# Depthwise products on 8 channels at four shifts, side by side on TensorE; natural channel order of x; the fractional part's transfers by halves

## The chip, the core and the metric

The kernel runs on one core of a Trainium2 chip. A core has five engines that run side by side and meet at semaphores: TensorE (matrix products; PE in the profile, its weight loads PEld), VectorE (DVE), ScalarE (ACT), GpSimd (POOL) and SyncE (SP), which here issues the transfers. Sixteen DMA engines move the data. SBUF is the working memory of 128 partitions; TensorE writes its results to PSUM, eight banks on the same 128 partitions. The metric is the device time of one execution in microseconds (us).

## The reference

The input `x` is 32 x 96 x 56 x 56 (images, channels, rows, columns), and two layers follow each other. Each layer works on its input normalised over groups of three channels (`_gn`) and is added to that input:

```
def _gn(v, G=32, eps=1e-5):
    g = v.reshape(B_, G, C_ // G, H_, W_)
    m = jnp.mean(g, axis=(2, 3, 4), keepdims=True)
    s = jnp.var(g, axis=(2, 3, 4), keepdims=True)
    return ((g - m) / jnp.sqrt(s + eps)).reshape(v.shape)
...
x = x + _L0_conv_ref(_gn(x), ...)
x = x + _L1_conv_ref(_gn(x), ...)
return x
```

The first layer is a quantised inverted bottleneck: a 1x1 convolution expands 96 channels to 576; batch normalisation and a 4-bit activation follow; then a depthwise 3x3 convolution (each of the 576 channels on its own, padding 1), the same two after it, and a 1x1 convolution back to 96 with batch normalisation. All three weights are quantised to 4 bits.

The second layer splits the channels into three parts of 32. The first part goes through a 3x3 convolution with gated weights, the second through a fractional Fourier transform over rows and columns, a gated 1x1 mix of real and imaginary parts, the inverse and the absolute value, the third through an ordinary Fourier transform with a gated mix and back. The parts are joined and go through a dense 3x3 convolution, 96 to 96.

## The kernel before

All images go through one program for the whole run; nothing is looped on the chip. For each image the code makes a list of steps in three streams: `head` (load, statistics, normalised input `hi`/`lo`), `body` (first layer) and `rest` (second layer). `arrange` interleaves the streams of neighbouring images, so that the second layer of image i stands beside the first layer of image i+1. `Order` then takes the recorded instructions, their true dependences, and a model of each instruction's duration (`Order.model`), and lays down a fixed order for each engine by list scheduling. The order on the chip is the result of that planner; DMAs are all issued by SP in such a fixed order too.

**First layer.** Pixels are held by parity: a channel's 56 x 56 plane is four planes of 28 x 28 (u = 0 to 3 for row and column parity), each with a border, 872 bytes (`QS`) in fp8. The 576 hidden channels come in five blocks (b) of 128, the last of 64.
- `expand(b, u)`, L684: four f32r products per parity into a PSUM pair of banks; `quant_act` (L633) has ScalarE apply scale, offset and relu to 8-bit codes, and VectorE shift and mask them in `q1s` (partition = channel).
- `leave(b, u)`, L702, writes `q1s` to DRAM (`sd`); `enter(b, h)`, L710, reads it back so that a partition is one of 32 channels x 4 parities: tile `d`, 128 partitions, two groups of 32 channels to a tile, three buffers.
- `depthwise(b, g)`, L718: for a group of 32 channels the 3x3 convolution on parity planes is a product with a 128 x 128 weight matrix (input parity and channel by output parity and channel) at four shifts of the plane: (0,0), (0,1), (1,0), (1,1). Four products of 392 columns accumulate in one bank; there are two halves. So 18 groups x 8 = 144 products per image, 4608 in all. ScalarE and VectorE quantise the pair of banks to `q2s`.
- `leave2` and `enter2` (L734, L741) take the result through DRAM (`gd`) to `q2`, channels on partitions, and `project(u)` (L744) makes the output and adds it to `x`.
The pool of PSUM pairs has two buffers, which expand, depthwise and project share.

**Second layer.** `norm` (L821) normalises the middle channels into a part of `F` and waits for the last product of the image before. `leave_x`/`enter_x` (L828, L832) turn that part through DRAM from channels on partitions to rows on partitions (`xh`). `forward_h`, `forward_w`, `inverse_w` and `inverse_h` are the transform; `leave_pq`/`enter_pq` (L984, L988) turn its result back into `F`, in one piece. `mix_f` (L1003) multiplies `F` by the gated weights: its products have 32 columns of weights, and for j = 0 to 3 write to PSUM partitions 32j to 32j + 31 of one bank. `mix_t` (L1065) does likewise. `spatial` (L1084) is the gated 3x3 convolution. The three parts meet in `cat`; `winograd` (L1106) and `final` (L1140, products on L1145) make the dense convolution and add it to `x`, and `store` (L1192) writes it out.

The channels of `x` lie on the partitions in the order 64 to 95, 32 to 63, 0 to 31 (`groups`, L441), so that `load` and `store` need three DMAs of 32 partitions for each quarter of a plane.

The products that the change is about:

```
for half in range(2):
    for t in range(4):
        nc.tensor.matmul(
            ps[:, half, :HN],
            dw[n][:, t, :],
            view(s["d"][b, g], PQ * (14 * half + t // 2) + t % 2, [[PQ, 14], [1, HH]]),
            start=(t == 0),
            stop=(t == 3),
        )
```

Of the kernel before, what the change touches and what calls it, by code (L numbers as in the profile page):

```python
# [63 lines left out]
NB = 5  # L65
# [74 lines left out]
class Order:  # L140
# [16 lines left out]
    def needs(self, tiles):  # L157
# [3 lines left out]
        for k, access in enumerate(self.access):  # L161
            for a, w in access:
# [10 lines left out]
                if m not in past:  # L173
                    past[m], free[m] = [], set()
                    if m in tiles:
                        pool, tag, bufs = tiles[m]
                        row = tags.setdefault((pool, tag), [])
                        if len(row) >= bufs:
                            free[m] |= users[row[-bufs]]
                        elif pool in ("p1", "p3"):  # L180
                            free[m] |= early
                        if row:
                            free[m].add(first[row[-1]])
                        first[m] = k
                        row.append(m)
# [19 lines left out]
    def model(self):  # L205
# [3 lines left out]
        for i, e, access in zip(self.ins, self.eng, self.access):  # L209
# [6 lines left out]
            if i.opcode == "DMACopy":  # L216
                took = 0.55 if e == "SP" else 0.4
                size = _bytes(outs[0].dtype)
                for _, c in outs[0].ap:
                    size *= c  # L220
                move = size / 200e3
                for a in (outs[0], ins[0]):
                    run = _bytes(a.dtype)
                    for step, c in reversed(a.ap):
                        if step * _bytes(a.dtype) == run or c == 1:
# [3 lines left out]
                    if run < 512:  # L229
                        move *= 1.4  # L230
                        break
                lag = 1.0 + move
            elif e == "PE":
# [7 lines left out]
                else:  # L241
                    took = max(cols / 2350.0, 0.05)
            elif e == "Activation":
# [177 lines left out]
def block_kernel(ctx: ExitStack, tc: tile.TileContext, out: bass.AP, a: dict):  # L421
# [19 lines left out]
    groups = ((0, 2 * G), (G, G), (2 * G, 0))  # L441
    xts = {}

    def load(i):
        xt = xp.tile([C, HW], F32, tag="x", name=f"x{i}")
        for at in range(0, HW, 2 * HN):
            for p, c in groups:
                src = x_in[i, c : c + G].rearrange("c h w -> c (h w)")
                nc.sync.dma_start(out=xt[p : p + G, at : at + 2 * HN], in_=src[:, at : at + 2 * HN])
# [12 lines left out]
    with tc.tile_pool(name="prep", bufs=1) as pp:  # L462
# [35 lines left out]
        eye = load_tmp("eye32")  # L498
        dw = []
        for g in range(NQ):  # L500
            d = cp.tile([128, 4, 128], FP8, tag=f"dw{g}", name=f"dw{g}")
            nc.vector.tensor_tensor(
                view(d.rearrange("p s m -> p (s m)"), 0, [[128, 4], [4, 32], [1, 4]]),
                view(w2, 16 * g, [[4, 4], [0, 32], [1, 4]]),
                view(eye, 0, [[0, 4], [1, 32], [0, 4]]),
# [59 lines left out]
    p1 = Pool(ctx.enter_context(tc.tile_pool(name="p1", bufs=1)), "p1", 1, tiles)  # L565
    p3 = Pool(ctx.enter_context(tc.tile_pool(name="p3", bufs=3)), "p3", 3, tiles)
# [78 lines left out]
    def layer0(i):  # L645
# [56 lines left out]
        def leave(b, u):  # L702

            n = blk(b) // 32
            if u == 0:
                s["sd", b] = dp.tile([n, 32, 4, QS], FP8, tag=f"sd{n}", name=f"sd{i}_{b}")
            q = q1s[(NB * i + b) % 2]
            nc.sync.dma_start(out=s["sd", b][:, :, u, :].rearrange("g c n -> c g n"), in_=q[: blk(b), u, :])

        def enter(b, h):  # L710

            d = p3.tile([128, 2, QS], FP8, tag="d", name=f"d{i}_{b}_{h}")
            src = s["sd", b][2 * h : 2 * h + 2].rearrange("g c u n -> (c u) g n")
            nc.sync.dma_start(out=d, in_=src)
            for g in range(2):
                s["d"][b, 2 * h + g] = d[:, g, :]

        def depthwise(b, g):  # L718
            n = 4 * b + g
            ps = pair(f"pd{i}_{n}")  # L720
            for half in range(2):
                for t in range(4):
                    nc.tensor.matmul(  # L723
                        ps[:, half, :HN],
                        dw[n][:, t, :],
                        view(s["d"][b, g], PQ * (14 * half + t // 2) + t % 2, [[PQ, 14], [1, HH]]),
                        start=(t == 0),
                        stop=(t == 3),
# [5 lines left out]
        def leave2(b, g):  # L734

            n = blk(b) // 32
            if g == 0:
                s["gd", b] = dp.tile([32, n, 4, 2 * HN], FP8, tag=f"gd{n}", name=f"gd{i}_{b}")
            nc.sync.dma_start(out=s["gd", b][:, g], in_=s["q", b, g])

        def enter2(b):  # L741
            nc.sync.dma_start(out=q2[b][: blk(b)], in_=s["gd", b].rearrange("c g u n -> (c g) u n"))
# [73 lines left out]
    def layer1(i):  # L816
# [11 lines left out]
        def leave_x():  # L828
            s["xd"] = dp.tile([G, HW], F32, tag="xd", name=f"xd{i}")
            nc.sync.dma_start(out=s["xd"], in_=s["F"][2 * G : 3 * G])  # L830

        def enter_x():  # L832

            s["xh"] = p1.tile([2 * H, G // 2, W], F32, tag="h", name=f"xh{i}")
            for q in range(2):
                src = s["xd"][G // 2 * q : G // 2 * (q + 1)].rearrange("c (h w) -> h c w", w=W)
                nc.sync.dma_start(out=s["xh"][H * q : H * (q + 1)], in_=src)

        def norm1():
# [3 lines left out]
            nc.vector.tensor_scalar(s["T"][:G], xts[i][:G], mean[:G], rstd[:G], ALU.subtract, ALU.mult)  # L843

        def norm0(u):
# [3 lines left out]
                view(xts[i][2 * G : C], W * (u // 2) + u % 2, [[2 * W, HH], [2, HH]]),  # L849
                mean[2 * G : C],  # L850
                rstd[2 * G : C],
# [116 lines left out]
        def inverse_h(g):  # L968
# [8 lines left out]
            if g < 4:  # L977
                dst = view(pq, 4 * W * g, [[2 * W, 2], [G // 2 * W, 2], [1, 2 * W]])
# [5 lines left out]
        def leave_pq():  # L984
            s["pd"] = dp.tile([2 * H, G + 1, W], F32, tag="pd", name=f"pd{i}")
            nc.sync.dma_start(out=s["pd"], in_=s["pq"])

        def enter_pq():  # L988
            for q in range(2):
                src = s["pd"][H * q : H * (q + 1)]  # L990
                nc.sync.dma_start(
                    out=s["F"][G * q : G * (q + 1)].rearrange("c (h w) -> c h w", w=W),
                    in_=src[:, :G, :].rearrange("h c w -> c h w"),
                )
                nc.sync.dma_start(
# [494 lines left out]
```

## Time and profile before

| | |
|---|---|
| median of 3 runs | 3622.18 us (3622.07 to 3627.27) |
| the profiled execution | 3621.32 us, its span 3619.5 us |
| VectorE, its two largest groups | L638: 232.5 us (640, mean 371 ns) and 150.3 us (576, mean 273 ns) |
| ScalarE, its two largest groups | L636: 628.9 us (640, mean 1003 ns) and 578.3 us (576, mean 1004 ns) |
| DMA | 406.08 MB in 491611 packets, mean 112 GB/s |
| granted TensorE clock | 0.947 of full speed, mean |

How to read the profile's lines: a group names its line in the code, the engine, the operation, output tiles <- input tiles, shapes, and the count; then its busy time (overlaps within the group counted once), the mean duration of one in ns, and the idle time of the engine just before them with what ended it. A TensorE record lasts until its result is written, so records of products that follow each other overlap; how long one holds the array is the distance to the next one's start. An f32 product stands in the records twice. In the timeline a row is a run of equal instructions: start, length from the first start to the last end, engine, line, operation, tiles, shapes, count.

### The profile page before, as it was taken

What the parts mean: (1) busy time and instruction counts of PE and PEld (TensorE: products, weight loads), DVE (VectorE), ACT (ScalarE), POOL (GpSimd) and SP (SyncE); (2) the same over time, 40 slices, a digit from 0 to 9 for tenths busy, and PEclk for the clock granted to TensorE, in tenths of its full rate; (3) what the DMA queues carried; (4) which work ended last, traced back from release to release, by engine and by line L of the source; (5) the groups of instructions that cost most, each with busy time, mean ns of one, the idle gap of its engine ahead of it and who ended that gap; (6) DMA issues with size and microseconds to landing.
All of it is one profiled execution on the core that took longest, in us unless ns stands there. A gap on an engine that the chain in (4) does not pass through costs nothing. (4 is left out here: it accounts for less than half of the span.)

```text
span 3619.5 us, 50492 instructions
## 1 busy us (share of the span) xinstructions
PE 3326.5 (92%) x17024; PEld 2059.6 (57%) x17024; DVE 2458.2 (68%) x5553; ACT 2109.3 (58%) x2792; POOL 584.3 (16%) x657
## 2 busy tenths in 40 slices
PE   3799999999999999999999999999999999999987
PEld 2555565556565555565555565555655555655554
DVE  6457676667667667667676766676676676766765
ACT  3566555566556566555566656566555665555542
POOL 3111110111101111101111101111101111101100
PEclk9899999999999999999999999999999999999997
DMA  4344444444454444444444444444444444444332
GB/s 109 103 120 120 113 121 112 108 123 113 116 123 112 106 124 112 115 123 103 108 124 114 118 122 103 114 123 113 117 123 102 118 119 110 124 112 107 101 91 48
DMA packets 491611, 406.08 MB, mean 112 GB/s; under 512 B 221094, under 2 KB 443288, under 8 KB 490328
## 3 DMA queue, kind: packets, MB, share of 16 engines
q1 hardware_dynamic: 487168, 400.10, 44.1%
q10 hardware_dynamic: 4184, 2.75, 0.3%
q8 instruction: 135, 2.21, 0.3%
q14 instruction: 124, 1.02, 0.1%
HBM read 202.71 MB, written 199.97 MB: 111 GB/s over the span
## 5 line engine op out<-in xcount | busy, mean ns | idle before, releaser
L723 PE MATMUL pd<-d,dw 128*128 128x392 fp8e4 x4608 | 1026.7, 358 | 62.8 <-DMA d<-sd 60.3
L636 ACT ACTIVATE q2s<-pd,o,s 128x784 uint8<-128x784 f32 x576 | 578.3, 1004 | 628.8 <-PE pd L723 620.2
L1145 PE MATMUL pc<-V,wcw 96*96 96x392 f32 x2304 | 887.3, 495 | 9.3 <-DVE V L1122 9.3
L636 ACT ACTIVATE q1s<-pe,o,s 128x784 uint8<-128x784 f32 (+1 forms) x640 | 628.9, 1003 | 285.1 <-PE pe L689 283.0
L723 PEld LDWEIGHTS <-dw 128*128 128x128 fp8e4 x4608 | 468.2, 104 | 551.5 <-issue 276.8
L689 PE MATMUL pe<-hi,w1r 96*128 96x392 f32 x1280 | 526.2, 415 | 97.8 <-ACT q1s L636 70.8
L1145 PEld LDWEIGHTS pc<-V,wcw 96*96 96x96 f32 x2304 | 374.7, 164 | 213.6 <-issue 173.2
L689 PE MATMUL pe<-lo,w1r 96*128 96x392 f32 x1280 | 471.1, 368 | 3.3 <-POOL lo L680 2.9
L638 DVE TENSOR_SCALAR q1s<-q1s 128x218 uint32<-128x218 uint32 (+1 forms) x640 | 232.5, 371 | 257.5 <-ACT q1s L636 252.1
L689 PEld LDWEIGHTS pe<-hi,w1r 96*128 96x128 f32 x1280 | 243.0, 192 | 237.9 <-ACT q1s L636 141.0
L638 DVE TENSOR_SCALAR q2s<-q2s 128x196 uint32<-128x196 uint32 x576 | 150.3, 273 | 238.0 <-ACT q2s L636 227.4
L680 POOL TENSOR_TENSOR lo<-v,hi 96x784 fp32r<-96x784 f32 x128 | 238.2, 1861 | 258.0 <-ACT hi L679 241.2
L689 PEld LDWEIGHTS pe<-lo,w1r 96*128 96x128 f32 x1280 | 246.7, 193 | 52.0 <-issue 16.8
L748 PE MATMUL pp<-q,w3q 128*96 128x392 fp8e4 x1280 | 244.0, 333 | 18.9 <-DMA q<-gd 8.3
L628 POOL TENSOR_TENSOR stb<-veb,mhalf 96x1 f32<-96x1 f32 x32 | 23.2, 726 | 1324.2 <-DVE veb L627 1324.2
L748 PEld LDWEIGHTS <-w3q 128*96 128x96 fp8e4 x1280 | 151.1, 124 | 107.5 <-issue 41.5
L679 ACT CAST hi<-v 96x784 fp32r<-96x784 f32 x128 | 107.7, 841 | 174.0 <-DVE v L676 173.3
L758 DVE SCALAR_TENSOR_TENSOR x<-pp,s,x 96x392 f32<-96x392 f32 x256 | 145.4, 617 | 72.9 <-PE pp L748 70.8
L1022 POOL COPY cat<-sq 32x392 f32<-32x392 f32 x256 | 144.9, 566 | 287.2 <-ACT sq L1018 278.7
L1088 PE MATMUL ps<-s,g 128*128 128x392 f32 x512 | 187.7, 502 | 0.0
L1102 ACT ACTIVATE cat<-ps,b 32x392 f32<-32x392 f32 x256 | 162.5, 636 | 16.3 <-PE ps L1088 12.1
L676 DVE TENSOR_SCALAR v<-x,sta 96x784 f32<-96x784 f32 x128 | 89.6, 700 | 101.3 <-POOL lo L680 79.9
(158 smaller groups left out, 4393.5 us busy)
## 6 DMA issues: line engine op xcount, KB each, us to landing
d<-sd SPq DMA_DIRECT2D x288, 218.0 KB
gd<-q2s SPq DMA_DIRECT2D x576, 98.0 KB
sd<-q1s SPq DMA_DIRECT2D x512, 109.0 KB
q<-gd SPq DMA_DIRECT2D x128, 392.0 KB
x<-in_x_dram SPq DMA_DIRECT2D x384, 98.0 KB
out_dram<-x SPq DMA_DIRECT2D x384, 98.0 KB
pd<-pq SPq DMA_DIRECT2D x32, 808.5 KB
F<-pd SPq DMA_DIRECT2D x64, 392.0 KB
```

Of the source, the lines that this page charges most:

```text
L636: nc.scalar.activation(dst, ps, AF.Relu, bias=offset, scale=scale)
L638: nc.vector.tensor_scalar(w, w, 4, 0x0F0F0F0F, ALU.logical_shift_right, ALU.bitwise_and)
L679: nc.scalar.copy(s["hi"][:, u, :], v)
L680: nc.gpsimd.tensor_tensor(s["lo"][:, u, :], v, s["hi"][:, u, :].bitcast(F32), ALU.subtract)
L689: nc.tensor.matmul(ps[:, half, :HN], w1[:, 128 * b : 128 * (b + 1)], part[:, u, HN * half : HN * (half + 1)], start=(n == 0), stop=(n == 1),)
L723: nc.tensor.matmul(ps[:, half, :HN], dw[n][:, t, :], view(s["d"][b, g], PQ * (14 * half + t // 2) + t % 2, [[PQ, 14], [1, HH]]), start=(t ...
L748: nc.tensor.matmul(ps[:C, half, :HN], w3[:, b * C : (b + 1) * C], q2[b][:, u, HN * half : HN * (half + 1)], start=(b == 0), stop=(b == NB ...
L758: nc.vector.scalar_tensor_tensor(part, src, A3, part, ALU.mult, ALU.add)
L1022: nc.gpsimd.tensor_copy(cat[G : 2 * G, r : r + 7, 1 : 1 + W], src)
L1088: nc.tensor.matmul(ps[:, :HN], s["g0"][:, 128 * t : 128 * (t + 1)], view(s0, PQ * (14 * half + t // 2) + t % 2, [[PQ, 14], [1, HH]]), star ...
L1102: nc.scalar.activation(dst, src, AF.Identity, bias=b0[2 * G : C], scale=1.0)
L1145: nc.tensor.matmul(ps[:C, :HN], wc[:, k, C * dx : C * (dx + 1)], V[:, :, dx : dx + W], start=(dx == 0), stop=(dx == 2),)
```

## The change

The depthwise product takes 8 channels at a time. A partition of `d` now is one of 8 channels x 4 input parities x 4 shifts, instead of 32 channels x 4 parities; the sum over the shifts happens in one product instead of in four that accumulate. A product's weights have 8 channels x 4 output parities = 32 columns, and the four products t = 0 to 3 of a half write to four different quarters of the PSUM partitions. The number of products, their 392 columns and their 128 rows stay.

To have the four shifts on partitions, `enter` reads each plane four times from DRAM, at the column shifts 0 and 1 in one DMA and the row shifts (y) in two DMAs of 64 partitions, in runs of 6944 bytes. `d` moves to a pool of its own with two buffers. `leave`, `leave2` and `enter2` follow with other DRAM layouts, `_groups` and `_taps` with other orders of channels and taps; the weight tiles shrink from 512 to 128 columns.

`x` keeps its natural channel order on the partitions: `load` and `store` take one DMA of 96 partitions instead of three of 32, and the second layer's parts are read from other partitions (`cat` keeps its order, so `wc` is reordered on its input side alone).

`leave_x`, `enter_x`, `leave_pq` and `enter_pq` come in two halves of 16 channels (pq: a third piece for its last column); a half of pq leaves after the second and the fourth `inverse_h`, the last piece after the fifth.

The planner's model changes in two places: a DMA's duration is made from the number and the length of its runs, and a product with 32 columns of weights counts 0.055 us. So the order on all engines is laid down anew.

```diff
@@ Order.model
-                size = _bytes(outs[0].dtype)
-                for _, c in outs[0].ap:
-                    size *= c
-                move = size / 200e3
...
+                    move = max(move, n * 0.0017 if run < 512 else math.ceil(n / 16) * max(0.05 + run / 43e3, run / 27e3))
...
                     took = max(cols / 2350.0, 0.05)
+                    if weights == G and cols >= HN:
+                        took = 0.055
@@ load (store likewise)
-            for p, c in groups:
-                src = x_in[i, c : c + G].rearrange("c h w -> c (h w)")
-                nc.sync.dma_start(out=xt[p : p + G, at : at + 2 * HN], in_=src[:, at : at + 2 * HN])
+            nc.sync.dma_start(out=xt[:, at : at + 2 * HN], in_=src[:, at : at + 2 * HN])
@@ weights
-            d = cp.tile([128, 4, 128], FP8, tag=f"dw{g}", name=f"dw{g}")
+            d = cp.tile([128, 4, 32], FP8, tag=f"dw{g}", name=f"dw{g}")
@@ leave
-                s["sd", b] = dp.tile([n, 32, 4, QS], FP8, tag=f"sd{n}", name=f"sd{i}_{b}")
+                s["sd", b] = dp.tile([4, 8, 4 * n, QS], FP8, tag=f"sd{n}", name=f"sd{i}_{b}")
             q = q1s[(NB * i + b) % 2]
-            nc.sync.dma_start(out=s["sd", b][:, :, u, :].rearrange("g c n -> c g n"), in_=q[: blk(b), u, :])
+            nc.sync.dma_start(out=s["sd", b][u], in_=q[: blk(b), u, :])
@@ enter
-            d = p3.tile([128, 2, QS], FP8, tag="d", name=f"d{i}_{b}_{h}")
-            src = s["sd", b][2 * h : 2 * h + 2].rearrange("g c u n -> (c u) g n")
-            nc.sync.dma_start(out=d, in_=src)
+            d = p4.tile([128, 8, QS], FP8, tag="d", name=f"d{i}_{b}_{h}")
+            n = 8 * QS - 32
+            src = s["sd", b][:, :, 8 * h : 8 * (h + 1), :].rearrange("u c g n -> (u c) (g n)")[:, :n]
+            flat = d.rearrange("p g n -> p (g n)")[:, :n]
+            (pitch, _), row = flat.ap
+            for y in range(2):
+                part = bass.AP(src.tensor, src.offset + PQ * y, [list(src.ap[0]), [1, 2], [1, n]])
+                dst = bass.AP(flat.tensor, flat.offset + pitch * y, [[2 * pitch, 64], list(row)])
+                nc.sync.dma_start(out=dst, in_=part)
             for g in range(2):
-                s["d"][b, 2 * h + g] = d[:, g, :]
+                s["d"][b, 2 * h + g] = d[:, 4 * g : 4 * g + 4, :]
@@ depthwise
                     nc.tensor.matmul(
-                        ps[:, half, :HN],
+                        ps[32 * t : 32 * (t + 1), half, :HN],
                         dw[n][:, t, :],
-                        view(s["d"][b, g], PQ * (14 * half + t // 2) + t % 2, [[PQ, 14], [1, HH]]),
-                        start=(t == 0),
-                        stop=(t == 3),
+                        view(s["d"][b, g][:, t, :], PQ * 14 * half, [[PQ, 14], [1, HH]]),
+                        start=True,
+                        stop=True,
                     )
@@ layer1
-        def leave_pq():
-            s["pd"] = dp.tile([2 * H, G + 1, W], F32, tag="pd", name=f"pd{i}")
-            nc.sync.dma_start(out=s["pd"], in_=s["pq"])
+        def leave_pq(g):
+            n = 16 if g < 2 else 1
+            s["pd", g] = dp.tile([2 * H, n, W], F32, tag=f"pd{g}", name=f"pd{i}_{g}")
+            nc.sync.dma_start(out=s["pd", g], in_=s["pq"][:, 16 * g : 16 * g + n, :])
...
-            S(leave_x, K("xd"), {K("norm"): 0.0}, sp=0.6),
-            S(enter_x, K("xh"), {K("xd"): 3.0}, sp=0.6),
-            S(leave_pq, K("pd"), {K("ih", 4): 0.0}, sp=0.6),
-            S(enter_pq, K("pq"), {K("pd"): 4.0}, sp=2.0),
+            *[S(lambda g=g: leave_x(g), K("xd", g), {K("norm"): 0.0}, sp=0.6) for g in range(2)],
+            *[S(lambda g=g: enter_x(g), K("xh", g), {K("xd", g): 3.0}, sp=1.1) for g in range(2)],
+            *[S(lambda g=g: leave_pq(g), K("pd", g), {K("ih", (1, 3, 4)[g]): 0.0}, sp=0.6) for g in range(3)],
+            *[S(lambda g=g: enter_pq(g), K("pq", g), {K("pd", g): 4.0}, sp=1.1) for g in range(3)],
```

## The prediction

> **What bounds the kernel now.** I read the page's totals first, then busy time by stage, the groups on TensorE, one tiled product in the timeline, and the DMA issues last.
>
> ```profile
> span 3619.5 us, 50492 instructions
> PE 3326.5 (92%) x17024; PEld 2059.6 (57%) x17024; DVE 2458.2 (68%) x5553; ACT 2109.3 (58%) x2792; POOL 584.3 (16%) x657
> ```
>
> The span split at the first and the last `norm` of the second layer (us; then PE, PEld, DVE, ACT and POOL busy; granted clock; DMA):
>
> ```profile
> 0.00:146.00 146.00, 74.94 (x314) 46.62 (x314) 78.40 (x207) 56.51 (x63) 46.88 (x31) 0.95 0.39 103
> 146.00:3529.00 3383.00, 3187.85 (x16450) 1975.28 (x16450) 2329.46 (x5250) 2027.03 (x2684) 531.49 (x613) 0.95 0.46 114
> 3529.00:3620.00 91.00, 63.76 (x260) 37.71 (x260) 50.34 (x98) 25.81 (x45) 5.92 (x13) 0.75 0.23 48
> ...
> L825 DVE TENSOR_SCALAR F<-x,stb x32: 1901/1904/1905, 146.3 to 3528.9; 32x3136 f32<-32x3136 f32 x32
> ```
>
> The middle holds 31 periods of 3383/31 = 109.1 us. In each, TensorE is busy 102.8 us and idle 6.3; VectorE is busy 75 and ScalarE 65. TensorE sets the period. What stands behind it: that each image's `norm` (L825) waits for the last product of the image before makes a serial chain; the last image, with little beside it, takes 3614 - 3529 = 85 us for it (first start of L825 there to the last L1190).
>
> ```profile
> L723 PE MATMUL pd<-d,dw 128*128 128x392 fp8e4 x4608 | 1026.7, 358 | 62.8 <-DMA d<-sd 60.3
> L1145 PE MATMUL pc<-V,wcw 96*96 96x392 f32 x2304 | 887.3, 495 | 9.3 <-DVE V L1122 9.3
> L1009 PE MATMUL pz<-F,g 98*32 98x392 f32 x1024 | 118.5, 510 | 8.1 <-DMA F<-pd 5.4 <-ACT cat L1102 1.3 <-DVE cat L1080 1.3
> ```
>
> L723 is the largest group. Its 1026.7 us count the tail of each run, which overlaps what follows. The old program's order has 907 unbroken runs of depthwise products; a product's record lasts 0.34 us where the array is held for 0.17 (below), so each tail is 0.17 and the path holds 1026.7 - 907 x 0.17 = 873 us. That is the sum's first term.
>
> **What the change does to TensorE.** The number of products stays 4608, but each has 32 columns of weights and its own quarter of the output partitions, so four could run at once. The trace has such a product: L1009 (`mix_f`), four at partitions 32j. Its rows, with a depthwise row for the price of a pass (start, us):
>
> ```profile
> 604.30 1.01 PE L723 MATMUL pd<-d,dw 128*128 128x392 fp8e4 x5
> ...
> 212.07 1.52 PE L1009 MATMUL pz<-F,g 98*32 98x392 f32 x16 [1.32 <-ACT cat L1102]
> ...
> 538.34 0.83 PE L1009 MATMUL pz<-F,g 98*32 98x392 f32 x4
> 539.10 0.45 PE L689 MATMUL pe<-hi,w1r 96*128 96x392 f32 x1
> 539.38 0.34 PE L689 MATMUL pe<-lo,w1r 96*128 96x392 f32 x1
> ...
> 540.46 0.34 PE L689 MATMUL pe<-lo,w1r 96*128 96x392 f32 x1
> 540.73 0.54 PE L1009 MATMUL pz<-F,g 98*32 98x392 f32 x4
> ```
>
> Row one: five products in 1.01 us, the last taking 0.34, so one per 0.67/4 = 0.17 us: one pass of 392 columns. Row two: 16 records of two passes (0.33 us each) would need 5.3 us in series; they end in 1.52 = 4 x 0.33 + tail. Four quarters do run together, and issue keeps up.
> The rest shows what it costs to go in and out. Out: the row of four ends at 539.17, so its last record (0.49 long) began at 538.68, and the next full-width product at 539.10, 0.42 later where 0.33 is due: 0.09 lost. The one behind it starts 0.28 later where L689 otherwise takes 0.18: 0.10 lost again (a full weight load that wasn't hidden; behind L1072 the next L748 loses only 0.04). In: 540.46 to 540.73 is 0.27 for a 0.18 product: 0.09 lost; and the first record of each burst is 0.025 longer. A round trip is 0.25 to 0.32 us; I take 0.285, because most neighbours are f32 with wide weights, like L689.
>
> The order of the new program (it carries no time) has 755 runs of depthwise products: 122 of one, 288 of two, 211 of three to nine, 134 of ten and more. Two of a set go in one pass, and a set broken by other work needs another. Walking each run with one product per quarter and pass gives 122 + 346 + 561 + 626 = 1655 passes, not the 1152 of perfect sets: 1655 x 0.17 = 281 us. Changes between full and quartered products, with those of L1009 and L1072, rise from 182 to 1866: 842 more round trips, x 0.285 = 240 us. Runs of one or two, mostly between two products of L1145, cost more than before: 410 x 0.285 = 117 us of going in and out, to save 576 - 468 = 108 passes (18 us).
> TensorE: -873 + 281 + 240 = -352 us.
>
> [...]
>
> **The other parts.**
> `enter`: each `d` tile was one DMA of 218 KB and becomes two of 64 x 6944 B = 434 KB, four times the bytes; buffers go from three to two. The profile page gives the rate: 400.10 MB took 44.1% of 16 engines, that is 400.10/(0.441 x 3619.5) = 0.251 MB/us. 288 x 650 KB more = 187 MB, +746 us of a capacity of some 3300: DMA goes from 44% to about 71%, no bound. A tile's own transfer grows from 0.87 to 3.5 us (at that rate; long rows may do better). With 9 tiles per image there is one per 11 us, so two buffers cover it on average. Today's exposure:
>
> ```profile
>   DMA d<-sd: 137.3, 68
> ...
> q1 hardware_dynamic: 487168, 400.10, 44.1%
> ...
> d<-sd SPq DMA_DIRECT2D x288, 218.0 KB
> ```
>
> Behind a late `enter` on SP stand `leave`, `leave2` and the chain's own transfers, so a late tile also delays ScalarE's next output buffer. I charge 0 to 4 us per image for that and for less filler work on TensorE while the chain waits, and take 2, nearer to no change, because today's 6.3 us of idle already include 68 such waits: 32 x 2 = +64 us.
> SP's issues: 288 more for `d`, 96 for `xd` and `xh`, 64 for `pd`, 64 for `F`; 256 fewer for each of `load` and `store`: 2688 in both programs, so SP's load is the same: 0.
> Halves of x and pq: the first half starts while the second is made. The last image waits 13 us from `norm` to its first forward product and as long from the last inverse to `mix_f`; the halves can take some 2 + 3 us out of the 85 us chain. Not on the path while TensorE sets the period: 0 us; if the chain bound, -5 us per image.
> Building the weights: 18 VectorE instructions of 0.677 us on 512 elements get 128 (about 0.3 by the slope between that row and the 392-element rows at 0.56): up to -7 us in the prologue, and fewer store issues at the end, up to -2. I take -4 for both. Channel order and offsets move no work: 0.
>
> Sum: 3619.5 - 352 + 64 - 4 = 3327.5 us of span; the profiled execution took 1.8 us more than its span (3621.32), and the median of the runs is 0.9 us above that: 3330.
>
> **Rivals.**
> *Cheap trips (0.14).* [...]
> *Another bound (0.17).* At 100 us per period the 85 us chain has to get through two engines 75 to 90% busy; today's contention stretches it from 85 to 109. If it sets a period of 106, the span is 146 + 31 x 106 + 88 = 3520.
> *Late tiles (0.06), the slow side.* PE at the first product of each `d` tile waits for the two DMAs, as there are two buffers and a landing of 3.5 us. With each of 288 tiles exposed by the added 2.6 us it is 3268 + 749 = 4017; it is slower than before from 352/288 = 1.22 us of exposure per tile. I put its time at 3700 (1.5 us). Against: one tile per 11 us.
> *Not side by side (0.03).* If fp8 quarters don't run together, 4608 passes stay: 3619.5 - 873 + 783 + 240 = 3770. Against: the L1009 row.
>
> **How the numbers follow.** My sum has 0.60. Predicted 3330. Its own bounds: below 3180, by the cheap trips; above, trips at 0.32 (+29), quarters issued 0.054 us apart as the small transposes of L1031 are (+75), and idle of 6 instead of 2 us (+128): 3560. The range reaches to just beyond the cheap trips and just beyond the middle of "another bound": 3150 to 3530, which leaves out both slow cases (0.09) and the outer parts of the others (about 0.1). A measurement here tells 0.2% (7 us) from no change. Faster 0.90, same 0.02 (between another bound and the slow cases), slower 0.08.
>
> **What would show it.** Right: the depthwise group near 520 us of held array including trips, a full-width product starting 0.09 late behind each run, a period near 100 us, idle of about 8 us in it. Wrong: records of one set that start 0.17 us apart (not side by side); waits of PE for `d` beyond 350 us (late tiles); TensorE below 88% with no DMA wait ahead (another bound); products behind a run that start on time (cheap trips).

## The result and the profile after

The changed kernel takes 3907.89 us (median of 4 runs, 3903.18 to 3912.95) against 3622.12 us for the kernel before: a ratio of 1.0789, 95% interval [1.0768, 1.0810], slower by 7.9 %. The prediction was 3330 us.

The page of the changed kernel (totals, then the granted clock in 40 slices):

```profile
span 3903.8 us, 50930 instructions
PE 3249.6 (83%) x17024; PEld 1831.3 (47%) x17024; DVE 2410.4 (62%) x5553; ACT 2097.0 (54%) x2792; POOL 588.4 (15%) x657
...
PEclk9798899888889888889888998888889889888887
```

TensorE is busy 77 us less than before and idle 654 us instead of 293. In the clock row 30 of the 40 slices are below 0.9; before the change only the second and the last were.

The span split at the first and the last `norm` (the columns as in the prediction), and the row of `norm` itself:

```profile
150.40:3818.20 3667.80, 3118.14 (x16420) 1750.51 (x16420) 2291.81 (x5252) 2013.21 (x2682) 542.64 (x613) 0.88 0.57 156
```
```profile
L834 DVE TENSOR_SCALAR F<-x,stb x32: 1902/1903/1904, 150.4 to 3818.2; 32x3136 f32<-32x3136 f32 x32
```

Prologue and last image together are 1 us shorter than before. The whole loss is in the 31 periods: 3667.8/31 = 118.3 us instead of 109.1, with the DMA engines busy 57 % of the time (71 % were expected).

The groups of TensorE that answer to those shown of before:

```profile
L1156 PE MATMUL pc<-V,wcw 96*96 96x392 f32 x2304 | 966.8, 537 | 41.1 <-DVE V L1133 41.1
...
L732 PE MATMUL pd<-d,dw 128*32 128x392 fp8e4 x4608 | 475.3, 399 | 331.3 <-DMA d<-sd 319.3 <-ACT q2s L639 6.9 <-ACT q1s L639 4.7
...
L1020 PE MATMUL pz<-F,g 98*32 98x392 f32 x1024 | 181.9, 708 | 32.7 <-DMA F<-pd 12.0 <-ACT cat L1093 6.7 <-DVE cat L1091 5.7
```

The depthwise products (L732) did become cheap: by the distances between starts they hold the array for 427 us instead of 876. But 331 us of idle time stand before them, and the products of the second layer (L1156, L1020), which the change doesn't touch, have longer records (537 ns in the mean instead of 495, and 708 instead of 510).

One image in the timeline of TensorE, from a wait for `d` to the end of `mix_f` (start, length; the idle time before in brackets):

```profile
1613.53 0.51 PE L732 MATMUL pd<-d,dw 128*32 128x392 fp8e4 x7
1618.66 1.50 PE L732 MATMUL pd<-d,dw 128*32 128x392 fp8e4 x16 [4.62 <-DMA d<-sd]
1620.09 0.48 PE L620 MATMUL pma<-mva,gmat 96*96 96x1 f32 x2
1620.43 2.96 PE L1099 MATMUL ps<-s,g 128*128 128x392 f32 x4
...
1633.58 0.51 PE L757 MATMUL pp<-q,w3q 128*96 128x392 fp8e4 x2 [2.14 <-DMA q<-gd]
1634.63 4.27 PE L1020 MATMUL pz<-F,g 98*32 98x392 f32 x22 [0.54 <-ACT cat L1093]
1638.83 3.11 PE L757 MATMUL pp<-q,w3q 128*96 128x392 fp8e4 x12
1641.88 0.86 PE L1020 MATMUL pz<-F,g 98*32 98x392 f32 x6
1642.78 3.52 PE L757 MATMUL pp<-q,w3q 128*96 128x392 fp8e4 x20
1646.22 0.85 PE L1020 MATMUL pz<-F,g 98*32 98x392 f32 x4
```

The reader is to see three things. A product of the first layer that waits 4.62 us for its tile stands in front of `spatial` (L1099), which belongs to the second layer, had its two inputs complete at 1611.4, and starts behind it, at 1620.43, as the planned order has it. The 32 products of `mix_f` need 12.4 us (1634.63 to 1647.07), because the planned order puts 32 products of `project` (L757) between them. And at this place the array runs at half speed (granted clock 0.5 from 1633.9 to 1640.8): 22 products of `mix_f` in 4.27 us are 0.19 us each, where the 16 that the prediction showed took 1.52 us, 0.095 each.

What ends the period, in the timeline of VectorE:

```profile
1702.87 0.56 DVE L1201 TENSOR_TENSOR x<-x,pc 96x392 f32<-96x392 f32 x1
1704.14 0.56 DVE L1201 TENSOR_TENSOR x<-x,pc 96x392 f32<-96x392 f32 x1 [0.72 <-PE pc L1156]
1704.62 0.15 DVE L632 TENSOR_TENSOR stb<-stb 96x1 f32<-96x1 f32 x1
1704.81 1.90 DVE L834 TENSOR_SCALAR F<-x,stb 32x3136 f32<-32x3136 f32 x1
```

The next image's `norm` (L834) starts 0.1 us after the last addition of `final` (L1201). The following table has the stages of this serial chain, from the start of one `norm` to the start of the next, worked out from the records of six of the kernels (e8 to e13 are described below): means over images 4 to 27, in us. `final` is counted to its last product. The last column but one is the sum, the last one is when the products of `project` of the next image end, counted from `norm`.

| kernel | norm to first forward | to last inverse | to first mix_f | to the end of its copies | to first final | final | to next norm | period | project ends |
|---|---|---|---|---|---|---|---|---|---|
| before | 13.6 | 17.2 | 15.1 | 18.1 | 4.5 | 41.0 | 0.0 | 109.4 | 44.9 |
| after | 10.1 | 18.5 | 19.3 | 23.2 | 5.6 | 41.1 | 0.7 | 118.5 | 59.5 |
| e8 | 13.6 | 16.1 | 24.0 | 17.5 | 0.6 | 35.2 | 0.3 | 107.2 | 53.7 |
| e11 | 10.5 | 22.2 | 14.8 | 15.4 | 5.1 | 41.9 | 0.7 | 110.7 | 59.7 |
| e12 | 10.9 | 23.0 | 15.3 | 27.7 | 3.7 | 40.8 | 0.6 | 122.1 | 58.2 |
| e13 | 11.7 | 16.3 | 15.4 | 19.1 | 0.9 | 40.8 | 2.0 | 106.2 | 54.8 |

In each of them the first layer of the next image is through `project` with 46 % of a period or more to spare, and `norm` begins when `final` ends, in the mean at most 2 us behind its last product. The halves of x bring 3.5 us (13.6 to 10.1), where the prediction had 2; those of pq, which it gave 3, bring nothing that the way from the last inverse to `mix_f` shows (15.1 before, 14.8 to 19.3 with them). The stages round `mix_f` lose 9.3 us (33.2 to 42.5).

That `norm` follows `final` is written in the program: its step names the last step of `final` of the image before (`(i - 1, 1, "c", 1, 5): 0.0`). By the code `norm` reads `x` and the statistics of its own image and writes `F`, and the last products that read the old `F`, those of `mix_f`, end 58 us (median) ahead of it in the kernel before. So the link looks like one of the program's own making and not one of data; no run took it out, and how long the chain would be without it is open.

By TensorE's records with their clock: 770 us of its busy time fall in stretches at half clock, 317 us before, so 227 us are lost to the clock; counted at full clock the work fell from 3149 to 2815 us. Work -335, clock +227, idle +361, and 31 us of busy time without a clock record: +284, the difference of the spans (3903.8 - 3619.5).

### The profile page after: what moved, and what is told of

It reads as the page before. It is cut to its first block, busy times and chain, and to the rows that moved or that the text cites. A ratio compares the mean times of both kernels' runs of the same rounds, so it can differ in the third digit from the quotient of the medians.

```text
span 3903.8 us, 50930 instructions
## 1 busy us (share of the span) xinstructions
PE 3249.6 (83%) x17024; PEld 1831.3 (47%) x17024; DVE 2410.4 (62%) x5553; ACT 2097.0 (54%) x2792; POOL 588.4 (15%) x657
## 5 line engine op out<-in xcount | busy, mean ns | idle before, releaser
L1156 PE MATMUL pc<-V,wcw 96*96 96x392 f32 x2304 | 966.8, 537 | 41.1 <-DVE V L1133 41.1
L732 PE MATMUL pd<-d,dw 128*32 128x392 fp8e4 x4608 | 475.3, 399 | 331.3 <-DMA d<-sd 319.3
L692 PE MATMUL pe<-hi,w1r 96*128 96x392 f32 x1280 | 548.0, 428 | 72.7 <-ACT q1s L639 44.8
L1156 PEld LDWEIGHTS pc<-V,wcw 96*96 96x96 f32 x2304 | 353.1, 171 | 360.7 <-issue 278.7
L732 PEld LDWEIGHTS <-dw 128*32 128x32 fp8e4 x4608 | 138.7, 104 | 751.0 <-issue 598.6
L757 PE MATMUL pp<-q,w3q 128*96 128x392 fp8e4 x1280 | 276.2, 365 | 88.1 <-DMA q<-gd 82.6
L757 PEld LDWEIGHTS <-w3q 128*96 128x96 fp8e4 x1280 | 163.7, 135 | 241.0 <-issue 164.6
L641 DVE TENSOR_SCALAR q1s<-q1s 128x218 uint32<-128x218 uint32 (+1 forms) x640 | 163.6, 279 | 118.5 <-ACT q1s L639 110.1
L1099 PE MATMUL ps<-s,g 128*128 128x392 f32 x512 | 221.4, 582 | 0.0
L1020 PE MATMUL pz<-F,g 98*32 98x392 f32 x1024 | 181.9, 708 | 32.7 <-DMA F<-pd 12.0
L1187 DVE TENSOR_TENSOR md<-mc,pc 96x392 f32<-96x392 f32 x128 | 71.4, 558 | 186.6 <-PE pc L1156 185.4
```

Source lines behind the costliest of these rows:

```text
L641: nc.vector.tensor_scalar(w, w, 4, 0x0F0F0F0F, ALU.logical_shift_right, ALU.bitwise_and)
L692: nc.tensor.matmul(ps[:, half, :HN], w1[:, 128 * b : 128 * (b + 1)], part[:, u, HN * half : HN * (half + 1)], start=(n == 0), stop=(n == 1),)
L732: nc.tensor.matmul(ps[32 * t : 32 * (t + 1), half, :HN], dw[n][:, t, :], view(s["d"][b, g][:, t, :], PQ * 14 * half, [[PQ, 14], [1, HH]]), ...
L757: nc.tensor.matmul(ps[:C, half, :HN], w3[:, b * C : (b + 1) * C], q2[b][:, u, HN * half : HN * (half + 1)], start=(b == 0), stop=(b == NB ...
L1020: nc.tensor.matmul(ps[G * j : G * (j + 1), :HN], s["g1"][: 3 * G + 2, G * q : G * (q + 1)], s["F"][:, 2 * HN * j + HN * h : 2 * HN * j + H ...
L1099: nc.tensor.matmul(ps[:, :HN], s["g0"][:, 128 * t : 128 * (t + 1)], view(s0, PQ * (14 * half + t // 2) + t % 2, [[PQ, 14], [1, HH]]), star ...
```

## The experiments

The letters of the theories are those of each expectation. "Ratio" is to the kernel before, run beside it.

**The parts of the change alone.** e1 has everything but the depthwise part (halves, channel order, the planner's new transfer durations; `enter`, `leave`, `depthwise` as before). e5 is e1 with the old durations, e4 the kernel before with the new ones:

```diff
@@ Order.model (e4; e5 the reverse)
-                move = size / 200e3
...
+                    move = max(move, n * 0.0017 if run < 512 else math.ceil(n / 16) * max(0.05 + run / 43e3, run / 27e3))
```

> The change without its depthwise part: natural channel order of x, transfers of x and pq by halves, the planner's new DMA durations, and the depthwise products as before (128 x 128, four accumulating, d tiles of 218 KB, three buffers). Theory A (the fourfold bytes of d make its tiles land late, TensorE waits and its clock falls): these parts cost nothing, 3560 to 3640 us, idle of PE near 293 us. Theory B (going in and out of quartered products costs more than the sum has): the same, 3560 to 3640. Theory C (halves, order and the planner's new durations do the harm): 3750 to 3900 us here too.

> The kernel before with one edit: the planner's DMA durations are those of the change; nothing that runs on the chip differs but the order. Theory D (the new durations are too short, so the fixed orders of the engines put work ahead of transfers that haven't landed): slower by 80 to 180 us, 3700 to 3800. Theory E (the transfers by halves or the channel order cost the time of the run without the depthwise part): same as before, 3600 to 3640.

> The change without its depthwise part, and with the planner's DMA durations of before: halves and natural channel order alone. Theory D: 3580 to 3640. Theory E: 3740 to 3780, as with the new durations.

e1: 3761.22 us, ratio 1.0388 [1.0373, 1.0404]. e4: 3626.36 us, 1.0013 [1.0001, 1.0024]. e5: 3643.71 us, 1.0055 [1.0039, 1.0072]. Half of the loss is there with no change to the depthwise. The halves and the channel order, with the order of instructions made for them, cost 0.55 %; the planner's other durations, which change nothing but that order, cost 118 us beside them and 0.13 % in the kernel before. So neither theory D (the durations) nor theory E (the halves) met both of its numbers: it takes the two together.

**Bytes, mode changes, buffers.** e2 is the changed kernel with two planes read in place of eight, all four products on the same plane. e3 is e2 with full-width products that accumulate (weights padded with zeros), so with no quarters and no change of mode for them. e10 and e15 are e2 and e3 with three buffers for `d`; e9 is the kernel before with two.

```diff
@@ enter, depthwise (e2, e3, e10, e15)
-            d = p4.tile([128, 8, QS], FP8, tag="d", name=f"d{i}_{b}_{h}")
-            n = 8 * QS - 32
+            d = p4.tile([128, 2, QS], FP8, tag="d", name=f"d{i}_{b}_{h}")
+            n = 2 * QS - 32
...
-                s["d"][b, 2 * h + g] = d[:, 4 * g : 4 * g + 4, :]
+                s["d"][b, 2 * h + g] = d[:, g : g + 1, :]
...
@@ depthwise (e3, e15)
-                        ps[32 * t : 32 * (t + 1), half, :HN],
+                        ps[:, half, :HN],
...
-                        start=True,
-                        stop=True,
+                        start=(t == 0),
+                        stop=(t == 3),
@@ pools (e10, e15)
-    p4 = Pool(ctx.enter_context(tc.tile_pool(name="p4", bufs=2)), "p4", 2, tiles)
+    p4 = Pool(ctx.enter_context(tc.tile_pool(name="p4", bufs=3)), "p4", 3, tiles)
```

> The changed kernel, but enter reads only two planes per partition instead of eight, 2 x 55 KB of long runs... 110 KB per DMA, 219 KB per tile as before the change, and the four products of a set all read the same plane (so the depthwise convolution takes the wrong channels). Instructions, products, quarters, two buffers and the number of DMAs stay. Theory A: the waits of PE for d fall from 440 us to below 150, the half-clock time with them, and the time to 3300 to 3420 us. Theory B: bytes are not the matter, 3750 to 3900 us. Theory C: 3750 to 3900 us. If the number of buffers and not the bytes makes tiles late: 3600 to 3800.

> As the run with a quarter of the bytes, but each product has 128 columns of weights, zero outside its own 32, and the four accumulate in one bank as before the change: no quarters, no going in and out (two planes per partition are read here too, so the depthwise convolution takes the wrong channels). Theory A: TensorE holds the array for depthwise as before (870 us), so the time is near that of before, 3580 to 3680 us, 250 to 330 slower than the run with quarters. Theory B: faster than the run with quarters, by 100 us or more. Theory C: as slow as the changed kernel.

> The kernel before, its input tiles d of the depthwise in a pool of their own with two buffers instead of three; nothing else. Theory F (the third buffer of d is what the changed kernel lacks): at least 3730 us, waits for d grow from 137 us to 300 us or more. Theories C and H: within 1 % of 3622 us, because a d tile lands in under 4 us and its products last 12 us before the change.

> The changed kernel with a quarter of the bytes in d (two planes read, all four products from the same plane, so the output is not the reference's), as in the run with quarter bytes at 3910 us, and three buffers for d instead of two. Theory F (two buffers make the loads late): 3760 us or less, waits for d under 200 us instead of 429 us. Theory C (the order of the work on the in-order engines makes the loss): within 1.5 % of 3910 us. Theory H: as C, and the time at half clock stays above 900 us.

> The run with a quarter of the bytes and full-width accumulating products (3982 us; the output is not the reference's), with three buffers for d instead of two. Its planner price is that of the kernel before, 0.167 us, close to the 0.17 us that the product takes. Theory F2 (at full width two buffers are too few, because a tile's products last 12 us): 3800 us or less. Theory C (neither buffers nor price; the two layers' interleaving round the chain's mix_f): within 1.5 % of 3982 us.

Each of these kernels also gets its own order from the planner (e2 has 1298 changes between full and quartered products, the changed kernel 1866), so a time here is that of the edit with its order.

e2: 3910.32 us, ratio 1.0797 [1.0767, 1.0827]. With a quarter of the bytes (a tile lands 3.65 us after its issue instead of 5.72, medians) the time is the same. The wait rows of L732, e2 first, then the changed kernel:

```profile
  issue: 562.3, 428
  DMA d<-sd: 561.6, 199
...
  DMA d<-sd: 439.9, 130
```

TensorE waits for `d` longer with the smaller load, 562 us instead of 440, so it isn't the length of the transfer that makes these waits long. That it is a late issue in its place is likely and not shown. e3: 3981.83 us, 1.0995 [1.0967, 1.1023]; without quarters and their mode changes the loss stays, so they aren't needed for it. That e3 is 71 us slower than e2 can't be put down to the missing quarters alone, as its order differs too. e9: 3618.43 us, 0.9999 [0.9989, 1.0008]. e10: 3897.39 us, 1.0771 [1.0740, 1.0802], as theories C and H had it. Two buffers aren't the cause in the kernel before nor in e2. At full width the third buffer, with the order that comes with it, is worth 88 us (e15: 3893.57 us, 1.0753 [1.0737, 1.0769]), half of what theory F2 asked, and the kernel is still slow: neither of the two theories met its number there.

**TensorE's load alone.** e8 is the kernel before with three of four depthwise products left out.

```diff
@@ depthwise (kernel before)
-                for t in range(4):
+                for t in range(1):
```

> The kernel before, in the old layout, with one of the four shifted products of each depthwise set left out three times over: 1152 products of 392 columns instead of 4608, so the second layer's filter has a quarter of its taps and the output is not the reference's. Loads, tiles, buffers, exits and the rest are as before; the planner prices the fewer instructions by its own rule. TensorE has 3456 x 0.19 us = 657 us less to do, more than the change can ever save, and there is no column tiling, no change of mode, no doubled load. Theory T (the prediction's own: TensorE's time sets the period): 3622 - 657 is about 2965 us, and not above 3150 even with 2 to 5 us an image of new idle time. Theory C (the period is the serial chain norm, forward, inverse, mix_f, final, norm of the second layer, which TensorE's backlog lengthens only where it stands inside the chain): the time falls by less than half of the 657 us, 3300 us or more, TensorE is busy under 85 % of the span, and the half clock that follows from idle time takes part of the gain back. Theory H (the clock gate alone makes the loss: with less to do, TensorE falls to half clock): the time is not under 3600 us, with the time at half clock above 900 us.

3564.41 us, ratio 0.9843 [0.9820, 0.9866]. Its totals and the split of its span:

```profile
PE 2985.8 (84%) x13568; PEld 1859.7 (52%) x13568; DVE 2405.8 (68%) x5553; ACT 2092.0 (59%) x2792; POOL 591.6 (17%) x657
```
```profile
142.80:3466.80 3324.00, 2859.88 (x13102) 1781.65 (x13102) 2281.08 (x5248) 2009.79 (x2684) 538.57 (x613) 0.89 0.45 116
```

The products left out, in the old layout, give 54 us. Counted at full clock TensorE has 560 us less to do than before (2589 us against 3149; the expectation's 657 was too much). The period is 3324/31 = 107.2 us, with TensorE busy 86 % of it: theory T, the prediction's own, falls. Theory H falls too, since 760 us at half clock (383 before) go with a faster kernel. The planner makes another order for this kernel as well, so 107.2 is one order's period, not the least that is possible.

**The order alone.** The kernels from here on, except e16, have the changed kernel's instructions; only numbers in the planner differ, and with "grouped" its rule that among the ready products one of the same tile goes next counts all products with 32 columns of weights (those of `mix_f` and `mix_t` too) as alike.

```diff
@@ Order.model (price; e16 likewise for the 128-column depthwise product of the kernel before)
-                        took = 0.055
+                        took = 0.13
@@ Order.model (grouped)
+            if e == "PE" and not i.is_transpose and _count(ins[1]) == G and _count(ins[0]) >= HN:
+                self.group.append("quarters")
+                continue
             self.group.append(outs[0].tensor.name if few else None)
```

> The changed kernel with the planner's DMA durations of before, so that a pair of d transfers counts 4.3 us instead of 2.1; the 0.055 us of a product stay. Changes between full and quartered products fall from 1866 to 866 in the new order. Theory D: PE's waits for d below 200 us, half-clock time below 500 us, 3250 to 3450. Theory F (two buffers and two DMAs per tile hold it back whatever the order): 3700 to 3900. Theory B (going in and out alone): 3600 to 3750.

> As the run before it, and the planner keeps quartered products together where it can (726 changes of mode, 1161 passes). Theory B: 150 us or more faster than without grouping. Theory D: 20 to 80 us faster. Theory F: 3700 to 3900.

> The changed kernel, only that its planner takes 0.13 us for a quartered product instead of 0.055 us (the trace has 0.093 us of array time for each of 4608, and a load of some 0.04 to 0.10 us more at each change of mode that it does not hide). Theory G (the planner's order is made for a depthwise that is too cheap, so products stand ahead of their data and the chain waits behind them): 3800 us or less, waits for d under 350 us instead of 440 us. Theory C without G (the interleaving of two layers on one in-order engine costs this whatever the price): within 1.5 % of 3908 us.

> The changed kernel with 0.20 us as the planner's price of a quartered product instead of 0.055 us (0.13 us gave 3699 us). Theory G (the price has to be what a product costs with its waits; 0.09 us of array time and its share of the mode changes are 0.13 to 0.15 us): 3680 to 3780 us, no better than 3699 us by much, since 0.20 us is too dear and lets chain work run ahead while the first layer falls behind. Theory L (the planner's order is a lottery, any price lands anywhere): no relation to the price, for example above 3850 us or below 3620 us.

> The changed kernel with 0.13 us as the price and with a planner that keeps quartered products together (about 870 mode changes in its order instead of 1658). Theory B2 (with the price right, the mode changes are the rest of the loss): 790 fewer changes at 0.09 to 0.14 us are 70 to 110 us of TensorE's time, and the time falls from 3699 us to 3640 us or less. Theory C (TensorE's load does not set the period): within 1.5 % of 3699 us, or slower, since grouped products hold chain products up for longer.

> The changed kernel with 0.13 us as the price and with the planner's old rule for transfer durations (200 GB/s; without the price this was 3983 us, against 3908 us with the new rule). Theory G (the price is the larger error and helps under either rule): at most 3850 us, that is 130 us or more under 3983 us. If the new durations made the rest of the loss, as they did where the halves alone were made (3644 us with the old rule, 3761 us with the new): under 3660 us. If the old rule is worse for the larger loads of d, as without the price: 3720 us or more.

> The kernel before, full width, old layout, old transfer durations; only its planner takes 0.055 us for a depthwise product instead of 0.167 us (the trace has 0.19 us for each). Theory G (a planner that believes the depthwise too cheap makes an order in which the chain's products stand behind it): at least 3700 us. Theory N (the wrong price hurts only together with the quartered layout and its late tiles): within 1.5 % of 3621 us.

> The changed kernel, quartered products kept together, price 0.10 us instead of 0.13 us. Theory G with B2 (grouping and a price near the cost are what counts): 3500 to 3620 us, below the kernel before or level with it. Theory L (lottery: an order that differs a little can land anywhere between 3535 and 4025 us): above 3650 us.

> The changed kernel, quartered products kept together, price 0.13 us, and the old rule for transfer durations. Theory G with B2: 3500 to 3700 us, since grouping took 164 us off with the new rule (3699 to 3535 us), and the old rule had 3756 us without grouping, so about 3590 us. Theory L: outside this, above 3750 us.

| durations | price | not grouped | grouped |
|---|---|---|---|
| new | 0.055 | 3907.89 (after), 1.0789 | |
| new | 0.10 | | 3752.66 (e17), 1.0370 [1.0345, 1.0394] |
| new | 0.13 | 3698.83 (e11), 1.0214 [1.0190, 1.0239] | 3534.59 (e13), 0.9759 [0.9743, 0.9774] |
| new | 0.20 | 4025.41 (e12), 1.1143 [1.1098, 1.1189] | |
| old | 0.055 | 3982.94 (e6), 1.0985 [1.0951, 1.1020] | 3901.18 (e7), 1.0771 [1.0754, 1.0787] |
| old | 0.13 | 3755.77 (e14), 1.0372 [1.0354, 1.0389] | 3867.43 (e18), 1.0686 [1.0667, 1.0705] |

The same instructions take 3535 to 4025 us. e11 has no fewer waits for `d` than the changed kernel (its row: 440.0 us in 162 waits, against 439.9 us in 130) and is 209 us faster:

```profile
  DMA d<-sd: 440.0, 162
```

So the sum of those waits tells nothing; theory G's number for them missed where its time was right. What counts is likely what stands behind a wait; the timeline above shows one such place, and no run singles it out. e13, the fastest, is 2.4 % faster than the kernel before:

```profile
PE 2985.8 (84%) x17024; PEld 1788.4 (51%) x17024; DVE 2389.8 (68%) x5553; ACT 2093.8 (59%) x2792; POOL 582.3 (16%) x657
```
```profile
143.20:3452.00 3308.80, 2858.64 (x16450) 1710.45 (x16450) 2271.28 (x5254) 2012.14 (x2684) 536.75 (x613) 0.90 0.61 173
```

Its period is 3308.8/31 = 106.7 us. Its timeline of TensorE at `mix_f` (L1023 here; `project` is L760):

```profile
1595.38 0.69 PE L760 MATMUL pp<-q,w3q 128*96 128x392 fp8e4 x2 [4.34 <-DMA q<-gd]
1596.23 5.46 PE L1023 MATMUL pz<-F,g 98*32 98x392 f32 x32 [0.17 <-issue]
1601.62 2.54 PE L760 MATMUL pp<-q,w3q 128*96 128x392 fp8e4 x12
1604.42 3.52 PE L760 MATMUL pp<-q,w3q 128*96 128x392 fp8e4 x20 [0.25 <-DVE x L770]
```

All 32 products of `mix_f` go in one run of 5.5 us, at 0.17 us each, where a product of it took 0.095 at full clock and 0.19 at half, and `project` follows behind them: the piece that took 12.4 us in the changed kernel. In the stage table e13 is 12.3 us per period below the changed kernel, of which `mix_f` with its way there and on gives 12.7 (48.1 to 35.4).

e16, with nothing of the change in it, is 3724.16 us, 1.0301 [1.0284, 1.0318]: a wrong price alone costs the kernel before 107 us (3616.77 for the kernel before beside it). Two of TensorE's groups there:

```profile
L725 PE MATMUL pd<-d,dw 128*128 128x392 fp8e4 x4608 | 983.3, 358 | 58.6 <-DMA d<-sd 53.1 <-ACT sq L1020 3.0 <-ACT q1s L638 1.6
...
L966 PE MATMUL pi<-e,cs 114*114 114x112 f32 x1088 | 133.3, 265 | 31.4 <-DVE cs L954 31.4
```

The depthwise is no dearer (1026.7 us busy before, 983.3 here); of the 79 us that TensorE is idle longer, 29 stand before the inverse transform (L966, 2.4 before the change of price) and 58 before the small products of the next image's statistics (78.1 us instead of 19.8).

Two rivals of the order can be judged from these runs. *The clock:* the mean granted clock is 0.945 in e1 and 0.948 in e16, where it is 0.947 in the kernel before, and both are slower; e4 has 0.981 and is no faster. *TensorE's own work:* counted at full clock, e18 has the least of the nine orders in the table, 2552 us, and takes 3867 us, where e13 has 2618 us and takes 3535. So e13's gain can't be put down to its fewer mode changes alone (theory B2, whose number it met): e18 has still fewer, 612 against 868.

What follows: the loss is one of order, since the same instructions in another order run faster than the kernel before. What does not follow is a rule for the numbers. A price of 0.13 instead of 0.055 takes 209, 227 and 34 us off in three pairs, but 0.20 is the slowest of all, and grouping, which takes 164 us off under the new durations at 0.13, adds 112 under the old. e6 lies above the ranges of all three of its theories, and e7 just outside each of its own. e14 met theory G's bound. e17 and e18 missed their ranges under theory G and met theory L's, and e12 met it as well, so e13 is one good order among the nine that were run, and I can't say that its numbers are the right ones. Which instruction the planner misjudges first, and what the time would be if the clock never fell, was not tried.

## Why the prediction was wrong

"TensorE sets the period" is the step that failed. 94 % busy was true of the period of before, but two things filled those 109 us: TensorE's work, and a serial chain that ran from `norm` to `norm` with no slack. The chain's 85 us were read from the last image, where it has the chip to itself, and were taken for a floor well out of reach; with another image's work between its products it takes 106 to 107 us in the fastest orders seen (e8, e13). Of the 352 us no order here got more than 84 (e13's span against that of before); whether another would is open. The parts of that term were sound: the work at full clock fell by 335 us, quarters run together (3 to 4 ns apart), and a round trip between full and quartered products, taken at 0.285 us, measures 0.28 (last section). One aside in it is miscounted: the runs of one or two had 122 + 576 = 698 products, so they save 230 passes and not 108; the sum doesn't use it. The bound below, 3180, leaves 0.19 us for a round trip; no run shows one so cheap, and the least that the changed kernel shows is 0.22 us (`mix_f` beside `project`).

The rival "another bound" had the mechanism and its price: a period of 106, 3520 us. e13 has 106.7 and 3535. But the changed kernel itself is 388 us slower than that: no rival foresaw an order that stretches the chain beyond its old length, and e13 came near 3520 only with a planner that was altered afterwards. The rival got 0.17, against the prediction's 0.60, though the prediction itself noted that `norm` waits for the image before. From the profile, the test was open: in the trace of before `project` of the next image ends 45 us into a 109 us period, and `norm` waits for `final` all the same.

The term of +64 us for "late `d` and less filler" was mis-sized: idle time grew by 361 us, and the lower clock took another 227, for which there was no term. "Laid down anew" stands in the description of the change, yet the sum had nothing for it: the halves were put at 0 us for their own cost, and e1 shows 141 us (3761.22 against 3620.44 for the kernel before beside it) from halves and new order together.

The rival "late tiles" named waits for `d`, and these did pass its mark of 350 us (440). Its price was wrong, because it came from the landing time: with a quarter of the bytes the time is the same (e2). "Not side by side" and "cheap trips" are out: the records of a set start together, and a full-width product behind a run starts 0.10 us late, where 0.09 was foretold. That DMA is no bound held (57 % busy), and prologue and end together gave 1 us where 4 were foretold (the first `norm` starts 4.1 us later, the last image is 5.0 us shorter). The 0 us for SP's issues was tested by no run.

Of the signs listed, the depthwise's array time of 427 us is under the 520 expected, but parts of each round trip fall on its neighbours and don't count in it; and "TensorE below 88% with no DMA wait ahead" was met by its first half only: there were DMA waits ahead, and another order of the same instructions is faster with waits as long (e11).

## What to carry to other kernels

Before costing work taken off the busiest engine, follow one image's serial chain through the trace and see whether its end starts the next: if so, the work counts only where it stands inside the chain, and an engine at 94 % can be a passenger. Where a planner lays down a fixed order, a new price in its model is a change in itself: run the old kernel with the new prices and the new kernel with a few others before judging the layout, for here the order alone moved the same instructions by 490 us. And a total of waits for a transfer says little until one has looked at what is queued behind each wait.

## What the runs showed of the hardware

Four fp8 products of a set, each on its own quarter of the output partitions, start 3 to 4 ns apart (medians of the distance) in the changed kernel (L732), and where sets follow each other at full clock one begins 0.18 us after the one before (median of 1342). In the kernel before each of the four full-width products takes that long: 0.17 us from start to start (L723, median of 3152). So four on their quarters cost about one pass.

A round trip between full and quartered products costs about 0.28 us at full clock, by distances between starts in the changed kernel (medians of some 440 cases each, products of `final`, L1156, as the neighbours). Going in, the first quartered product starts 0.42 us after one of L1156, where the next of L1156 starts after 0.33. Going out, the first of L1156 starts 0.27 us after the last set, where the next of a plain run of fp8 products starts after 0.17 (L757), and the one behind it 0.41 us later instead of 0.33. That is 0.09 + 0.10 + 0.08. With `mix_f` (L1020) beside `project` (L757) it is 0.09 going in (0.26 instead of 0.17, 58 cases), and going out 0.09 (0.42 instead of 0.33) and 0.04 (0.20 instead of 0.17, 25 cases), together 0.22.

The granted clock is either 1.0 or 0.5 in both traces: 383 us at half clock before, 966 us in the changed kernel, with TensorE still busy 83 % of the span. At half clock the products of L1156 start 0.65 us apart (median) instead of 0.33. In the changed kernel the clock falls 121 times. The longest idle gap between TensorE's records in the 10 us ahead of a fall has a median of 2.3 us and is 4.1 us at most; in the mean 28 % of those 10 us are idle, against 17 % of the span (before: 56 falls, a median of 1.75 us and at most 4.9 us, 19 % against 8 %). Ahead of 24 of the 121 there is no gap of 1 us, so these figures give no rule for when it falls.
